# Turned score blocks in layer 2, a last batch with tiles of its own, and dilation counts emitted beside layer 0's end

## The chip, the cores and the metric

One Trainium2 chip, one of its cores. A core has five engines that run side by side, each with a queue that it works off in order: PE (TensorE: matrix products and transposes into PSUM), DVE (VectorE), ACT (ScalarE), POOL (GpSimd) and SP (SyncE, used here to issue loads). Engines wait for each other through semaphores. The metric is the time of one execution on the device, in microseconds, median of several runs.

## The reference

Four layers over a graph with 16 batches of N = 1024 nodes and D = 128 features. Each layer's result is added to its input, and the sum is normalised over the features (mean and variance, epsilon 1e-5).

```python
# layer 0: attention over the symmetrised scores
h = x @ W_w.T + W_b
e = einsum('bjl,bkl->bjk', h @ A, h); e = e + swapaxes(e, 1, 2)
att = softmax(where(adj > 0, e, -9e15), axis=1) * adj
h_prime = relu(att @ h)
coeff = sigmoid(concat([x, h_prime]) @ gate_w.T + gate_b)
return coeff * x + (1 - coeff) * h_prime
# layer 1: dilation (rows one after the other: a row with more than 10 neighbours
# loses those whose rank is a multiple of sf, and the columns likewise), then three
# SAGE convolutions with batch norm on the dilated matrix, and a linear layer on all three
# layer 2: scores as in layer 0 with other weights, but masked with 0:
att = softmax(where(adj > 0, e, 0), axis=1) * adj
h_prime = relu(att @ h)          # three gates i, f, o over concat([x, h_prime])
return o * tanh(sigmoid(i * h_prime + f * x))
# layer 3: two graph convolutions
h = elu(elu(x @ W0 + b0))
norm_A = dinv[:, :, None] * (adj + I) * dinv[:, None, :]   # dinv = (row sum of adj + I) ** -0.5
h = elu(norm_A @ (h @ W1) + b1)
return norm_A @ (h @ W2) + b2
```

As e is symmetric, its block (j, i) is the transpose of block (i, j); the mask is symmetric too.

## The kernel before

P = 128 partitions; a batch's 1024 nodes are NT = 8 row blocks. A [128, 1024] product is made in H2 = 2 halves of 512 columns[...]. The work of one batch is cut into streams, Python generators that emit instructions and pause. `in_rounds` (L816) takes the streams of one round in turns; `yield n` lets a stream pause for n turns. So the order of each engine's queue is mostly written by the pauses, and a scheduler settles the rest and sets the semaphores. A tile's memory is given again to a later tile; the later writer then waits for the last reader.

**Layer 0** (to about 640 us) has three streams in a round: `before(b+1)` loads the adjacency, writes it to fp8 tiles Y (named carry in the trace) that stay on the chip, and sums rows into `deg` (L932); `attention(b)` makes, per row block, a mask (msk, L981), the scores (`wide_matmul`, L724), a reduce that adds the mask and takes the minimum into `mx0` (L984), exp (L986), the scaled rows hs (L990), and, one row block late, the weighted sum acc (L974); `after(b-1)` makes the gates (L1002 to L1011), the mix, the norm (`normed`) and the store to x1_d (L1020, on POOL's queue). After the last round, `after(15)` is emitted alone.

**The dilation** (layer 1's first part) goes through 8 row blocks x 2 groups of 8 batches. `prepare` (L1059) counts neighbours with matmuls (L1078) in two chunks of 4 batches and leaves sk, l1 and past (L1080 to L1084) on DVE; `fixed_point` (L1089) makes 6 evaluations (thr L1101, mid L1106 on DVE, counts pd L1109 on PE, ti L1113), which settle the removed entries of the diagonal block; `removal` (L1142) then works batch by batch on the other columns (first matmul L1153, keep L1157, carry L1166 on ACT). Its pools are opened after layer 0's are closed. Between the first two `prepare` and the loop stand a few operations on layer 0's statistics (L1187 to L1196): mx0 compared and reduced to nomem, deg + 1, its power -1/2 on POOL (dinv is another name for deg), a transpose on PE (L1193), the copy dt and a store. `zeros` is another name for mx0 (L681): layer 2 writes its counts of masked entries there.

**Layer 1's convolutions** follow (to about 1680 us); of their weights, ws (Wr + Wx, in `take_norm`) is touched by the new order.

**Layers 2 and 3** run as one pipeline. In round b: `convolve(b-2)` (layer 3), `mix(b-1)` (layer 2's gates and norm), `attention(b)`, `before(b+1)` (layer 1's linear layer, norm and layer 2's projections). `attention` (L1654), per row block: msk on ACT (L1668), which also sums the mask into zeros, scaled on DVE (L1669); scores on PE (L724); the reduce (add mask, maximum, L1673) from PSUM to em; nmx = -max (L1675); exp in place (L1677); a sum with the masked entries' share (L1680), its reciprocal (L1682), hs (L1684); and, one row block late, acc on PE (L1660). `convolve` (L1726): adjacency copied to fp32r tiles (L1735 ACT, L1745 DVE), transposes of x (x3T, L1739), product with U0 and two elus, then twice: product with U (L1592), split in high and low part (zhi, zlo), product with the adjacency (`propagated`, L1605, DVE L1607). At its end the result is turned back, added (L1771), normalised and stored (L1777, POOL's queue; SP's for the last batch). `before` loads the batch's rows (xn, L1258), makes yT and yn, adds (L1635), normalises, turns (xT, L1640) and multiplies (hT L1644, G L1648, hn L1651). After the rounds `convolve(14)` then `convolve(15)` run as one chain beside `mix(15)`.

A norm is bn_stats (L794) and bn_aggr (L796) on DVE, a power on POOL (L745), one small DVE operation (L799), and ACT's scaling (L801).

Of the kernel before, what the change touches and what calls it, by code (L numbers as in the profile page):

```python
# [9 lines left out]
F32 = mybir.dt.float32  # L10
# [12 lines left out]
P = 128  # L23
# [5 lines left out]
GB = 8  # L29
# [610 lines left out]
def fast_kernel(ctx: ExitStack, tc: tile.TileContext, t: dict, out: bass.AP, flag: bass.AP):  # L640
# [121 lines left out]
    def products(psum, *pairs):  # L762

        for p, c, _ in halves(psum):
            for i, (W, x) in enumerate(pairs):
                nc.tensor.matmul(p, W, x[:, c], start=(i == 0), stop=(i == len(pairs) - 1))  # L766
            yield p, c
# [118 lines left out]
    with ExitStack() as ph:  # L886

        early = ph.enter_context(tc.tile_pool(name="l0_early", bufs=1, reuse_waits="tile"))
        wts = ph.enter_context(tc.tile_pool(name="l0_w", bufs=1, reuse_waits="tile"))
        ps_w = ph.enter_context(tc.tile_pool(name="l0_pw", bufs=2, space=PSUM, reuse_waits="tile"))  # L890
        ps_a = ph.enter_context(tc.tile_pool(name="l0_pa", bufs=1, space=PSUM, reuse_waits="tile"))
        ps_h = ph.enter_context(tc.tile_pool(name="l0_ph", bufs=2, space=PSUM, reuse_waits="tile"))

        with tc.tile_pool(name="l0_raw", bufs=1) as raw:
            W0 = matrix(raw, t["L0_gnn_W_w"], "l0W")
            W0T = transposed(wts, ps_h, W0, "l0WT", "h")
            As0 = symmetric(raw, ps_h, matrix(raw, t["L0_gnn_A"], "l0A"), "l0As", "h")
            AW = raw.tile([P, P], F32, name="l0AW")
            p = ps_h.tile([P, P], F32, name="wtr", tag="h")
            nc.tensor.matmul(p, As0, W0, start=True, stop=True)  # L900
            nc.vector.tensor_copy(AW, p)
            M0 = wts.tile([P, P], F32, name="l0M")
            p = ps_h.tile([P, P], F32, name="wtr", tag="h")
            nc.tensor.matmul(p, W0, AW, start=True, stop=True)
            nc.vector.tensor_copy(M0, p)
            nu = wts.tile([P, 1], F32, name="l0nu")
            p = ps_h.tile([P, 1], F32, name="wtr", tag="h")
            nc.tensor.matmul(p, AW, column(raw, t["L0_gnn_W_b"], "l0b"), start=True, stop=True)
            nc.vector.tensor_scalar(nu, p, -1.0, None, op0=OP.mult)
        work = ph.enter_context(tc.tile_pool(name="l0_work", bufs=1, reuse_waits="tile"))  # L910
        small = ph.enter_context(tc.tile_pool(name="l0_small", bufs=2, reuse_waits="tile"))
        b0 = row_bcast(wts, t["L0_gnn_W_b"], P, "l0brow")
        gw = wts.tile([P, 2, 32], F32, name="l0gw")
        nc.vector.memset(gw, 0.0)
        with nc.allow_non_contiguous_dma(reason="a vector of 256"):
            nc.sync.dma_start(gw[:, :, 0], t["L0_gnn_gate_w"].rearrange("o (h d) -> d (o h)", d=P))
        gb = row_bcast(wts, t["L0_gnn_gate_b"], 1, "l0gb")
        gbh = wts.tile([P, 1], F32, name="l0gbh")
        nc.vector.tensor_scalar(gbh, gb, 0.5, None, op0=OP.mult)
        nbig = wts.tile([P, 1], F32, name="l0nbig")  # L920
        nc.vector.memset(nbig, BIG)

        def before(s, b):

            s.xn = work.tile([P, NT, P], F32, name="xn", bufs=3)
            nc.sync.dma_start(s.xn, nat(t["x"][b]))
            yield 1
            for it in range(NT):
                c = b * NT + it
                an = early.tile([P, N], F32, name="an", bufs=3)  # L930
                nc.sync.dma_start(an, t["adj"][b][it * P:(it + 1) * P, :])
                nc.scalar.activation(Y[b][:, it, :], an, AF.Copy, accum_out=deg[:, c:c + 1], saturate=False)  # L932

                chk = early.tile([P, N], FP8, name="chk")
                done = (it + 1) * P
                if done < N:
                    nc.vector.scalar_tensor_tensor(chk[:, done:], an[:, done:], 0.0, an[:, done:], op0=OP.is_gt,
                                                   op1=OP.not_equal, accum_out=other[:, b, it:it + 1], saturate=False)
                for h in range(it // 4 + 1):
                    js = range(4 * h, min(4 * h + 4, it + 1))  # L940
                    k = slice(js[0] * P, (js[-1] + 1) * P)
                    pt = ps_h.tile([P, 512], F32, name="pt", tag="h")
                    for i, jt in enumerate(js):
                        nc.tensor.matmul(pt[:, i * P:(i + 1) * P], Y[b][:, jt, it * P:done], identb, start=True, stop=True)
                    nc.vector.scalar_tensor_tensor(chk[:, k], pt[:, :k.stop - k.start], 0.0, an[:, k], op0=OP.is_gt,
                                                   op1=OP.not_equal, accum_out=other[:, b, 7 + it + 4 * h:8 + it + 4 * h],
                                                   saturate=False)
                if it == 2:
                    s.xT = work.tile([P, N], F32, name="xT", bufs=2)
                    for p, c, _ in turned(ps_h, s.xn):  # L950
                        nc.scalar.copy(s.xT[:, c], p)
                elif it == 4:
                    s.G = work.tile([P, N], F32, name="G", bufs=2)
                    for p, c in products(ps_h, (M0, s.xT)):
                        nc.scalar.activation(s.G[:, c], p, AF.Identity, scale=-1.0, bias=nu)
                    pz = gates(ps_h, early.tile([P, N], FP8, name="chk").bitcast(F32), (gw[:, 0, :], s.xT))
                    s.gx = small.tile([P, NT], F32, name="gx")
                    nc.vector.tensor_copy(s.gx.rearrange("p (q t) -> p q t", t=2), pz[:, :, :, 0])
                elif it == 5:
                    s.hn = work.tile([P, N], F32, name="hn")  # L960
                    for p, c, blocks in halves(ps_h):
                        for i, k in enumerate(blocks):
                            nc.tensor.matmul(p[:, i * P:(i + 1) * P], s.xT[:, k * P:(k + 1) * P], W0T, start=True, stop=True)
                        nc.vector.tensor_add(tiles3(s.hn[:, c]), tiles3(p), b0[:, None, :].to_broadcast([P, 4, P]))
                yield 2
            nc.gpsimd.dma_start(adj8_d[b], Y[b].bitcast(F32))

        def attention(s, b):
            s.acc = ps_a.tile([P, N], F32, name="acc")

            def weigh(jt, hs, em):
                for h in range(H2):
                    c = slice(h * 512, (h + 1) * 512)
                    nc.tensor.matmul(s.acc[:, c], hs, em[:, c], start=(jt == 0), stop=(jt == NT - 1))  # L974

            for jt in range(NT):
                js = slice(jt * P, (jt + 1) * P)
                c = b * NT + jt
                mn = mx0[:, c:c + 1]
                msk = work.tile([P, N], BF16, name="msk", bufs=2)  # L980
                nc.scalar.activation(msk, Y[b][:, jt, :], AF.Identity, scale=-BIG, bias=nbig)  # L981
                e = wide_matmul(ps_w, s.G[:, js], s.xT)
                em = work.tile([P, N], F32, name="em", bufs=2)
                nc.vector.tensor_tensor_reduce(em, e, msk, 1.0, 3.0e38, op0=OP.add, op1=OP.min, accum_out=mn)  # L984
                sm = small.tile([P, 1], F32, name="sm")
                nc.scalar.activation(em, em, AF.Exp, scale=-1.0, bias=mn, accum_out=sm)  # L986
                rs = small.tile([P, 1], F32, name="rs")
                nc.vector.reciprocal(rs, sm)
                hs = small.tile([P, P], F32, name="hs")
                nc.vector.tensor_scalar(hs, s.hn[:, js], rs, None, op0=OP.mult)  # L990
                yield
                if jt:
                    weigh(*late)
                late = jt, hs, em
                yield
            weigh(*late)
            yield

        def after(s, b):

            hpT = work.tile([P, N], F32, name="hpT")
            nc.scalar.activation(hpT, s.acc, AF.Relu)  # L1002
            yield 3
            pz = gates(ps_h, work.tile([P, NT, P], F32, name="r").rearrange("p t d -> p (t d)")[:, :N // 4], (gw[:, 1, :], hpT))
# [29 lines left out]

# [802 lines left out]
```

## Time and profile before

| what | value |
| --- | --- |
| three runs | 2775.41, 2781.0, 2783.75 us, median 2781.0 |
| the profiled execution | 2779.18 us, its span 2777.5, mean granted TensorE clock 0.978 |
| busy share of the span | PE 93%, DVE 77%, ACT 72%, POOL 12% |
| f32 matmuls of layer 2's scores (L724, G by hT) | 512 records, 593 ns each, 245.0 us |
| reduce of layer 2 (L1673) | 128, 1221 ns each, 156.3 us |
| mask of layer 2 (L1668) | 128, 1150 ns each, and 128 accumulator reads of 192 ns (median) |
| first removal of the dilation | 664.45 us |
| first scores of batch 15 in layer 2 | 2623.35 us |

A line of a timeline or of the page reads: engine, source line, operation, output tile <- input tiles, partitions x elements and type, count; in brackets the time that the engine was idle before it, and what ended that. PE's durations overlap, as matmuls are pipelined: the distance of two starts is what one costs in a full stretch. In the page's section of slices, a digit is the busy share of 1/40 of the span in tenths, and PEclk is the granted clock likewise.

### The profile page before, as it was taken

What the parts mean: (1) busy time and instruction counts of PE and PEld (TensorE: products, weight loads), DVE (VectorE), ACT (ScalarE), POOL (GpSimd) and SP (SyncE); (2) the same over time, 40 slices, a digit from 0 to 9 for tenths busy, and PEclk for the clock granted to TensorE, in tenths of its full rate; (3) what the DMA queues carried; (4) which work ended last, traced back from release to release, by engine and by line L of the source; (5) the groups of instructions that cost most, each with busy time, mean ns of one, the idle gap of its engine ahead of it and who ended that gap; (6) DMA issues with size and microseconds to landing.
All of it is one profiled execution on the core that took longest, in us unless ns stands there. A gap on an engine that the chain in (4) does not pass through costs nothing.

```text
span 2777.5 us, 41717 instructions
## 1 busy us (share of the span) xinstructions
PE 2586.3 (93%) x14808; PEld 1670.4 (60%) x14808; DVE 2131.3 (77%) x5905; ACT 1991.0 (72%) x3316; POOL 334.0 (12%) x287
## 2 busy tenths in 40 slices
PE   7999999995899879998999998999999999999985
PEld 3545444443666658877788894455555555555554
DVE  5888777876999967776788775777778777777865
ACT  6888888974888776666655445877777777777754
POOL 0000000030000002211122141011111111111100
PEclk9999999997999989999999998999999999999998
DMA  5555545520000052233467572111111111121000
GB/s 186 164 162 172 177 161 166 175 89 12 2 2 2 2 219 92 97 117 123 155 235 249 174 267 84 60 62 61 61 61 61 61 61 61 66 68 72 27 20 25
DMA packets 120810, 285.37 MB, mean 103 GB/s; under 512 B 12304, under 2 KB 65424, under 8 KB 113424
## 3 DMA queue, kind: packets, MB, share of 16 engines
q1 hardware_dynamic: 101280, 203.33, 22.3%
q0 software_dynamic: 19312, 79.28, 7.4%
q8 instruction: 119, 1.95, 0.3%
q14 instruction: 99, 0.81, 0.1%
HBM read 202.72 MB, written 79.82 MB: 102 GB/s over the span
## 4 chain that ended last, share of the span: by engine, by line
PE 40%; DVE 19%; ACT 9%; issue 9%; POOL 4%; DMA 3%; POOLq 0%; DVEq 0%; ACTq 0%; SPq 0%
PE pmm L724 6%; PE ph L1605 6%; PE acc L1315 5%; PE acc L1660 5%; PE ph L766 3%; PE ph L759 3%; ACT xn L801 3%; PE acc L974 2%; PE ph L1441 2%; POOL rn L745 2%; DVE em L1673 2%; DVE mid L1106 2%; PE ph L1592 2%; DVE ln_st L794 1%; PE s L1153 1%
## 5 line engine op out<-in xcount | busy, mean ns | idle before, releaser
L745 POOL TENSOR_TENSOR ln_rstd<-ln_rstd,mhalf 128x8 f32<-128x8 f32 (+1 forms) x68 | 121.6, 1788 | 1361.7 <-DVE ln_rstd L742 938.0
L724 PE MATMUL pmm<-xT,G 128*128 128x512 f32 x512 | 261.8, 604 | 0.0
L974 PE MATMUL acc<-em,hs 128*128 128x512 f32 x512 | 260.1, 607 | 1.3 <-DVE hs L990 1.1
L1315 PE MATMUL acc<-a,lo 128*128 128x512 f32 x768 | 240.0, 397 | 17.9 <-DVE lo L1282 17.9
L1660 PE MATMUL acc<-em,hs 128*128 128x512 f32 x512 | 248.6, 601 | 8.1 <-DVE hs L1684 7.8
L724 PE MATMUL pmm<-G,hT 128*128 128x512 f32 x512 | 245.0, 593 | 0.0
L1315 PE MATMUL acc<-a,hi 128*128 128x512 f32 x768 | 240.6, 398 | 3.0 <-ACT hi L1281 2.8
L801 ACT ACTIVATE xn<-xn,ln_nb,ln_rstd 128x128 f32<-128x128 f32 x512 | 205.0, 485 | 48.7 <-DVE ln_nb L799 48.7
L1668 ACT ACTIVATE msk<-A,nbig 128x1024 bf16<-128x1024 fp8e4 x128 | 147.1, 1150 | 73.7 <-DVE mx L1673 48.8
L986 ACT ACTIVATE em<-em,mx 128x1024 f32<-128x1024 f32 x128 | 146.8, 1147 | 59.6 <-DVE mx L984 59.2
L1315 PEld LDWEIGHTS acc<-a,lo 128*128 128x128 f32 x768 | 144.0, 190 | 54.6 <-DVE lo L1282 25.0
L984 DVE CUSTOM_DVE_ANT_0 em<-pmm,msk 128x1024 f32<-128x1024 f32 x128 | 156.3, 1221 | 23.2 <-PE pmm L724 22.4
L1673 DVE CUSTOM_DVE_ANT_0 em<-pmm,msk 128x1024 f32<-128x1024 f32 x128 | 156.3, 1221 | 11.6 <-PE pmm L724 11.3
L1315 PEld LDWEIGHTS acc<-a,hi 128*128 128x128 f32 x768 | 143.4, 190 | 33.1 <-ACT hi L1281 3.7
L1166 ACT ACTIVATE carry<-pc,negone 128x1024 fp8e4<-128x1024 f32 x128 | 141.0, 1115 | 24.4 <-PE pc L1165 19.9
L1605 PE MATMUL ph<-A,zhi 128*128 128x512 f32 x512 | 151.8, 438 | 1.5 <-ACT zhi L1595 1.3
L932 ACT ACTIVATE carry<-an 128x1024 fp8e4<-128x1024 f32 x128 | 134.7, 1052 | 25.9 <-DMA an<-in_adj 25.3
L1677 ACT ACTIVATE em<-em,nmx 128x1024 f32<-128x1024 f32 x128 | 146.2, 1142 | 8.1 <-DVE nmx L1675 7.8
L1660 PEld LDWEIGHTS acc<-em,hs 128*128 128x128 f32 x512 | 90.8, 191 | 92.7 <-issue 69.9
L981 ACT ACTIVATE msk<-carry,l0nbig 128x1024 bf16<-128x1024 fp8e4 x128 | 145.9, 1140 | 0.0
L1304 ACT CAST a<-carry 128x1024 fp32r<-128x1024 fp8e4 x96 | 99.5, 1050 | 50.4 <-PE acc L1315 50.3
L1304 ACT CAST a<-A 128x1024 fp32r<-128x1024 fp8e4 x96 | 99.2, 1050 | 50.3 <-PE acc L1315 50.3
(319 smaller groups left out, 6236.5 us busy)
## 6 DMA issues: line engine op xcount, KB each, us to landing
an<-in_adj SPq DMA_DIRECT2D x128, 512.0 KB, 3.7
adj_d<-carry POOLq DMA_DIRECT2D x16, 1024.0 KB, 4.2
A<-dil_d SPq DMA_DIRECT2D x16, 1024.0 KB, 5.5
rdeg<-rdeg_d SPq DMA_DIRECT2D x32, 512.0 KB, 3.8
A<-adj_d SPq DMA_DIRECT2D x16, 1024.0 KB, 4.8
ag_d<-ag POOLq DMA_DIRECT2D x24, 512.0 KB, 5.2
ag<-ag_d SPq DMA_DIRECT2D x24, 512.0 KB, 5.4
xn<-in_x SPq DMA_DIRECT2D x16, 512.0 KB, 4.3
```

What stands on the lines that cost most here:

```text
L724: nc.tensor.matmul(p[:, h * 512:(h + 1) * 512], lhsT, rhs[:, h * 512:(h + 1) * 512], start=True, stop=True)
L745: nc.gpsimd.tensor_tensor(r, r, mhalf[:, :n], op=OP.pow)
L801: nc.scalar.activation(r[:, k.start + i, :], r[:, k.start + i, :], AF.Identity, scale=rstd[:, i:i + 1], bias=nb[:, i:i + 1])
L974: nc.tensor.matmul(s.acc[:, c], hs, em[:, c], start=(jt == 0), stop=(jt == NT - 1))
L984: nc.vector.tensor_tensor_reduce(em, e, msk, 1.0, 3.0e38, op0=OP.add, op1=OP.min, accum_out=mn)
L986: nc.scalar.activation(em, em, AF.Exp, scale=-1.0, bias=mn, accum_out=sm)
L1304: nc.scalar.copy(a, A[:, 2 * i:2 * i + 2, c])
L1315: nc.tensor.matmul(acc, part[:, jt, :], pieces[h * NT // 2 + i][:, j, :], start=(jt == 0 and p == 0), stop=(jt == NT - 1 and p == 1))
L1605: nc.tensor.matmul(p, part[:, jt, :], A[:, jt, c], start=(jt == 0 and i == 0), stop=(jt == NT - 1 and i == 1))
L1660: nc.tensor.matmul(s.acc[:, c], hs, ex[:, c], start=(jt == 0), stop=(jt == NT - 1))
L1668: nc.scalar.activation(msk, s.A8[:, jt, :], AF.Identity, scale=BIG, bias=nbig, accum_out=zs)
L1673: nc.vector.tensor_tensor_reduce(em, e, msk, 1.0, 0.0, op0=OP.add, op1=OP.max, accum_out=mx)
```

## The change

Three edits.

**Scores.** In layer 2, row block jt multiplies only the columns from (jt - 1) x 128 on. The blocks further left are turned by PE from the masked scores of earlier row blocks, which now stay in two tiles em0 and em1 (even and odd rows, at offsets `starts`). As block and mask are turned together, signs change: G is copied with scale -1, the mask is 0 or +BIG, the reduce takes the minimum, and exp writes to tiles of its own, ex. The mask's sums are gone: zeros is computed once as N - deg, in the dilation's setup. yn has one buffer in place of two; zn, x3T and prop share one tile.

```diff
-                zs = zeros[:, i:i + 1]
-                nc.scalar.activation(msk, s.A8[:, jt, :], AF.Identity, scale=BIG, bias=nbig, accum_out=zs)
-                nc.vector.tensor_scalar(zs, zs, -1.0 / BIG, None, op0=OP.mult)
-                e = wide_matmul(ps_w, s.hT[:, js], s.G)
-                em = wide("em", 3)
-                mx = small.tile([P, 1], F32, name="mx")
-                nc.vector.tensor_tensor_reduce(em, e, msk, 1.0, 0.0, op0=OP.add, op1=OP.max, accum_out=mx)
-                nmx = small.tile([P, 1], F32, name="nmx")
-                nc.vector.tensor_scalar(nmx, mx, -1.0, None, op0=OP.mult)
+                nc.scalar.activation(msk, s.A8[:, jt, :], AF.Identity, scale=-BIG, bias=nbig)
+                e = ps_w.tile([P, N], F32, name="pmm", tag="w")
+                at = max(lo - P, 0)
+                for c in ([slice(at, 512)] if at < 512 else []) + [slice(max(at, 512), N)]:
+                    nc.tensor.matmul(e[:, c], s.hT[:, js], s.G[:, c], start=True, stop=True)
+                for it in range(jt - 1):
+                    nc.tensor.transpose(e[:, it * P:(it + 1) * P], ems[it % 2][:, starts[it] + lo:starts[it] + lo + P], identf)
+                row = ems[jt % 2][:, starts[jt]:starts[jt] + N]
+                mn = small.tile([P, 1], F32, name="mn")
+                nc.vector.tensor_tensor_reduce(row, e, msk, 1.0, 0.0, op0=OP.add, op1=OP.min, accum_out=mn)
                 sm = small.tile([P, 1], F32, name="sm")
-                nc.scalar.activation(em, em, AF.Exp, bias=nmx, accum_out=sm)
+                ex = wide("ex", 2)
+                nc.scalar.activation(ex, row, AF.Exp, scale=-1.0, bias=mn, accum_out=sm)
...
             s.G = wide("G", 2)
             for p, c in products(ps_h, (As2, s.hT)):
-                nc.scalar.copy(s.G[:, c], p)
+                nc.scalar.activation(s.G[:, c], p, AF.Copy, scale=-1.0)
```

**The end of layer 0.** Layer 0's pools are split: `scores` (early and ps_w) closes after the last attention, `ending` after `after(15)`. The dilation's pools open in between, on the right side, and its first two `prepare` and first `fixed_point` are emitted in one round with `after(15)`. The loop starts at 1.

```diff
-        in_rounds([after(state[B - 1], B - 1)])
+    scores.close()
...
-        for s in steps[:G2]:
-            for _ in prepare(*s):
-                pass
+        in_rounds([chain(*(prepare(*s) for s in steps[:G2]), fixed_point(*steps[0])), after(state[B - 1], B - 1)])
+        ending.close()
+        ps_c = ph.enter_context(tc.tile_pool(name="dl_pc", bufs=2, space=PSUM, reuse_waits="tile"))
 
         nc.vector.tensor_scalar(mx0, mx0, 1.0e15, None, op0=OP.is_gt)
         nc.vector.tensor_reduce(nomem, mx0, AX.X, OP.max)
 
+        nc.vector.tensor_scalar(zeros, deg, -1.0, float(N), op0=OP.mult, op1=OP.add)
         nc.vector.tensor_scalar(deg, deg, 1.0, 1.0, op0=OP.add, op1=OP.max)
         nc.gpsimd.tensor_tensor(dinv, deg, mhalf[:, 0:1].to_broadcast([P, BT]), op=OP.pow)
...
-        for i in range(len(steps) + 1):
+        for i in range(1, len(steps) + 1):
```

**The last batch.** A class `Place` names where a batch's layer 3 has its tiles and PSUM: the usual ones, or, for batch 15, those that other streams no longer need, and the PSUM pool of the scores. The rounds run to b = 14, and one last round holds the rest. The pauses are changed: `before` from 1, 3, 7, 1, 4 to 2, 1, 5, 1, 1, `mix`'s last from 5 to 7, and shorter ones for batch 15.

```diff
+        class Place:
+            usual = dict(x="x3T", zhi="zhi", zlo="zlo", dB="dB", e="ehi", eb=2, psum=ps_h, ptag="h")
+            spare = dict(x="yT", zhi="hb2", zlo="yn", dB="em0", e="ex", eb=2, psum=ps_w, ptag="w")
...
+            def adjacency(self):
+                if not self.last:
+                    A = work.tile([P, NT, N], F32R, name="A")
+                    return [A[:, jt, :] for jt in range(NT)]
+                tags = [("hb0", 1), ("hb1", 1), ("hT", 2), ("G", 2), ("hn", 2), ("hT", 2), ("G", 2), ("hn", 2)]
+                return [self.of(f"A{jt}", tag, bufs, F32R) for jt, (tag, bufs) in enumerate(tags)]
...
-        for b in range(B):
+        for b in range(B - 1):
...
-        ends = [chain(convolve(state[B - 2], B - 2), convolve(state[B - 1], B - 1)), mix(state[B - 1], B - 1)]
-        in_rounds(ends)
+        in_rounds([chain(attention(state[B - 1], B - 1), mix(state[B - 1], B - 1), convolve(state[B - 1], B - 1)),
+                   mix(state[B - 2], B - 2),
+                   chain([2], convolve(state[B - 3], B - 3), convolve(state[B - 2], B - 2))])
```

## The prediction

> **What bounds the kernel.** I read the page's 40 slices first, for where an engine is full; then windows of single rounds of layers 2 and 3; then the timeline at the two places where the slices dip.
>
> ```profile
> PE   7999999995899879998999998999999999999985
> ...
> PEclk9999999997999989999999998999999999999998
> ```
>
> One slice is 69.4 us. PE is at 9 nearly everywhere, at full clock; it dips in slice 10 (625 to 694, the seam between layer 0 and the dilation) and in the last two. The change touches just these three regions: the rounds, the seam, the tail. A round of layers 2 and 3, start to start of the same instruction (columns: stretch, length, busy us and count of PE, PEld, DVE, ACT, POOL, then clock, DMA share, GB/s):
>
> ```profile
> 2087.15:2151.20 64.05, 63.57 (x251) 37.16 (x251) 50.17 (x155) 48.48 (x95) 7.06 (x4) 1.00 0.19 66
> 2281.30:2345.40 64.10, 63.63 (x251) 37.22 (x251) 50.23 (x155) 48.55 (x95) 6.75 (x4) 1.00 0.19 66
> ```
>
> PE is busy 63.6 of 64.1 us; DVE 50.2, ACT 48.5. So a round is TensorE time: what PE is spared shortens it, unless a wait appears; what DVE and ACT are spared buys slack only.
>
> **Part 1, scores of layer 2.** In each batch's attention 28 blocks lie under the diagonal. The 7 next to it stay matmuls, the other 21 become transposes of masked blocks kept in em0 and em1. Prices are start-to-start distances in a crowded stretch, since the recorded duration of one matmul overlaps the next:
>
> ```profile
> 2176.43 0.60 PE L759 MATMUL ph<-identf,xn 128*128 128x128 f32 x4
> 2176.87 1.02 PE L724 MATMUL pmm<-G,hT 128*128 128x512 f32 x2
> 2177.73 0.64 PE L759 MATMUL ph<-identf,xn 128*128 128x128 f32 x4
> ```
>
> The x2 of L724 are one 512-column matmul (512 records on the page for 16 batches x 8 row blocks x 2 halves): 0.86 us, 0.215 per 128 columns. Four transposes take 0.44, so 0.109 each. Removed 21 x 0.215 = 4.5 us, added 21 x 0.109 = 2.3: **-2.2 us of PE per batch**.
>
> A rule speaks against this. The Trainium skill, "TensorE: Matmul & The Clock Gate", Part 4 (PE-mode transpose), gives about 275 ns for a 128x128 transpose in a kernel and says that transposes don't by themselves engage the full clock. By it the 21 would cost 5.8 us: +1.3 per batch instead of -2.2. The trace has the same 275 ns as each record's duration (275 mean of L759 over the rounds), but starts 0.109 apart, and the clock of the windows, with 48 transposes in each round, is 1.00. I take 0.109; the new transposes too stand among matmuls, 1 to 6 in a row.
>
> DVE loses 8 x (0.147 for L1669 + 0.148 for L1675) = 2.4 us per round, ACT 8 x 0.193 of accumulator reads = 1.5. Both have over 13 us of slack: nothing, save that the chain from reduce to hs gets 0.15 shorter. Turning signs (min for max, scale -1 on exp and on G's copy) keeps forms and sizes: nothing. The separate ex tiles take exp's output out of em: nothing.
>
> **Stalls in the new round.** The change also moves the streams' pauses, and yn has one buffer for two. In the queue order of the changed kernel, DVE's add onto the next batch's rows (L1635 before) now stands ahead of hs of the third row block; before, three hs were ahead of it. The add waits for a buffer's turn: convolve's result is stored out of it, then the next rows are loaded into it (POOL, SP's queue, DVE):
>
> ```profile
> 2186.09 1.17 POOL L1777 DMA_DIRECT2D out<-xn  x1 [3.73 <-ACT xn L801]
> ...
> 2191.57 0.37 SPq L1258 DMA_DIRECT2D xn<-x_d  x1
> ...
> 2197.80 1.23 DVE L1635 TENSOR_TENSOR xn<-xn,yn 128x1024 f32<-128x1024 f32 x1 [2.59 <-DMA xn<-x_d]
> ```
>
> Store 5.5 us, load 6.2; the add comes 25.2 us after convolve's last product ends (near 2172.6). Add, statistics and aggregation (1.23 + 1.64 + 0.63) and the sums to hs follow: hs of block 2 at 28.7 to 30.5 on that clock, while PE's new queue, added up at the prices above, wants it at 29.0. So 0 to 1.5 us of stall per round, and about 1 at the round's first acc, against some 0.5 that PE idles now (64.05 - 63.57). Ends per round: -2.2 (all covered), 0 (everything eaten). I take -1.5 for each of the 15 rounds, **about -23**; the sixteenth batch's scores are counted in the tail.
>
> **Part 2, the seam.** Before, the dilation's first work waits for after(15)'s store, since its tiles reuse memory:
>
> ```profile
> 648.37 0.16 DVE L1081 SCALAR_TENSOR_TENSOR l<-s,off 128x4 f32<-128x4 f32 x1 [6.47 <-DMA x_d<-xn]
> ...
> 648.85 1.31 PE L1078 MATMUL s<-step,carry 128*128 128x128 bf16 x32 [16.02 <-DVE past L1084]
> ...
> 664.45 1.25 PE L1153 MATMUL s<-step,carry 128*128 128x512 bf16 x4
> ```
>
> PE idles 16 us from 632.8 on, and the first removal starts at 664.45. The change gives the dilation memory of its own on the right side and runs prepare and the six evaluations beside after(15). Taken alone, the evaluations (2.10 us apart: 657.82, 659.92 ...) could end some 15 us earlier. But an operation on POOL, deg to the power of -1/2, is moved with it:
>
> ```profile
> 584.47 20.75 POOL L1191 TENSOR_TENSOR deg<-deg,mhalf 128x128 f32<-128x128 f32 x1
> ```
>
> Before, deg + 1 (L1190) ran early, POOL's 20.75 us were hidden beside attention, and PE turned deg (L1193) at 626.4. Now zeros = N - deg is written over mx0 first, after nomem has read it, which needs the last row block's minimum, and deg + 1 stands behind it on DVE. The last hs is at 626.8; the four small operations (0.2 each) put deg + 1 near 628.5, and the power runs to about 649.5. Three queues stand behind it. PE: the transpose of deg comes right after prepare's second chunk; behind it after(15)'s gates, chunks 3 and 4, all counts. DVE: dt waits for that transpose, behind it all evaluations. POOL: after(15)'s rstd. So work restarts at 649.7, with 6 x 2.10 = 12.6 us of evaluations plus about 9 of after(15) and the last chunks on DVE, of which 2.5 fit in the evaluations' gaps (0.47 each): 19, first removal at 668.8, **+4.5**. One more wait: layer 1's sum of weights is now in DVE's queue within the dilation's first step, and its loads on SP stand behind one that waits for after(15)'s later store (near 680). Between 0 and +3; I take +1.5. Seam: **+6**. If the power were hidden after all, -12; if both waits fall worst, +9. After that step the instructions are in the same order as before.
>
> **Part 3, the tail.** From the first score of batch 15 (2623.35) to the end is 154.2 us. Before, convolve(14), mix(15), convolve(15) share tiles and PSUM (windows as above, then PE's timeline):
>
> ```profile
> 2680.00:2700.00 20.00, 12.30 (x58) 7.83 (x58) 10.14 (x32) 10.97 (x20) 3.07 (x2) 0.73 0.07 26
> ...
> 2720.00:2740.00 20.00, 7.80 (x31) 5.25 (x30) 11.96 (x36) 14.00 (x26) 3.57 (x3) 0.80 0.15 53
> ```
>
> ```profile
> 2738.88 3.55 PE L1592 MATMUL ph<-U,ehi 128*128 128x128 f32 x16 [7.88 <-DVE ehi L1579]
> ...
> 2763.53 0.66 PE L759 MATMUL ph<-identf,prop 128*128 128x128 f32 x4 [1.10 <-ACT prop L1768]
> ```
>
> PE is idle 7.7 and 12.2 us in these windows, some 39 from 2680 on. In the new order batch 15 has tiles and PSUM of its own and runs straight through, with mix(14), convolve(13) and (14) filling in. I add up: first score to last acc 47 us (59 before, because convolve(13)'s last product moves behind it and the scores save 2.2); mix(15) and convolve(15) up to U1, 36 (before 56.7: 2682.2 to 2738.88); then PE is full with both batches' products, 7.35 us each, to +76; and about 20 for the last transposes, norm and store (14.0 before, from 2763.53; batch 14 isn't finely split). 47 + 76 + 20 = 143: **-11**, ends -3 (the chains don't overlap where I assume) and -20 (half the idle time filled).
>
> **Sum.** -23 + 6 - 11 = -28 from the profiled execution's 2779.2 (span 2777.5): 2751. The runs shown have a median of 2781.0, 1.8 above, within their spread.
>
> **Rivals.** Under 0.3% (8.3 us) a measurement of this kernel can't be told from no change.
> A. *As summed*: 2751, own range 2740 to 2766. Chance 0.67.
> B. *The seam isn't blocked*, or the stalls vanish: POOL's power runs early after all, and the seam gains 12 where I count a loss of 6: 2751 - 18 = 2733. For it: the whole gap is one memory wait. Against: the queue order above. 0.20.
> C. *The saved PE time becomes waiting*: the rounds stay at 64 because hs sets the pace: 2779 + 6 - 11 = 2774, no change. For it: the 2.59 us wait at L1635. Against: DVE and ACT have 13 us of slack. 0.08.
> D. *Slower*: those rows arrive later, and PE waits at acc of block 2 in each round. This is a loop: a late round makes the store late again. With 4 us of stall, +1.8 net per round, 15 x 1.8 + 6 - 11 = +22: 2801. It decides from a stall of 2.2 + 5/15 = 2.5 us per round, that is, if the rows land 2.5 us later than I place them. Against: the turn's times are steady (12 rounds within 66.1). 0.05. The skill's transpose price would make it 2779 + 15 x 1.3 + 6 - 7.5 (the tail less its 3.5) = 2797; I count it in here.
>
> Range: 2726 to 2768, from B's far side to half of C. Faster 0.90, same 0.06, slower 0.04.
>
> **What would show it.** Right: rounds of 62.5 to 63 us, PE busy near 61.4; the power on POOL (L1191 before) starting near 628 with PE's transpose of deg after it; first removal at 667 to 672; 140 to 148 us from batch 15's first score to the end. Wrong: DVE idle before the add and PE idle at acc of block 2 by over 1.5 us a round (C, D); four transposes over 0.86 us apart; the first removal before 655 (B).

## The result, and the profile after

The changed kernel takes 2733.9 us (median of 5 runs, 2728.7 to 2735.6) against 2781.0 before: ratio 0.9827, 95% interval 0.9811 to 0.9843, so 47 us less. Forecast were 2751 as the likeliest and 2726 to 2768 as the range. The profiled execution of after has a span of 2732.4 us, 45.1 less than before's 2777.5. Cut at the same instructions of both traces (the first removal of the dilation; the first reduce of batches 0, 3 and 15 in layer 2), the 45.1 are:

| stretch | before | after | difference | forecast |
| --- | --- | --- | --- | --- |
| start to the first reduce of batch 0 (holds the seam) | 1720.8 | 1727.6 | +6.8 | +6 |
| batch 0 to batch 3 | 134.1 | 131.8 | -2.4 | -4.5 |
| batch 3 to batch 15, 12 rounds | 771.3 | 739.1 | -32.2 | -18 |
| first reduce of batch 15 to the end | 151.2 | 133.9 | -17.3 | -11 |

**Rounds.** Windows of two rounds of after (columns as in the prediction), then the whole list of PE's waits in after between 1860 and 2590: total us, times, longest:

```profile
2105.90:2167.50 61.60, 61.28 (x267) 38.31 (x265) 48.89 (x140) 47.83 (x87) 5.86 (x4) 1.00 0.20 69
2290.70:2352.30 61.60, 61.29 (x267) 38.31 (x265) 48.88 (x140) 47.83 (x87) 5.86 (x4) 1.00 0.20 69
```

```profile
PE acc L1678 <- DVE hs L1705: 3.5, 12, 0.3
```

Before, a round took 64.28 us in the mean of 12, between 63.6 and 66.1; now eleven of the twelve take 61.60 to 61.63, and the last 61.46. Over the 12 rounds PE is busy 2.3 us less per round (63.60 to 61.28), about what the turned blocks promised, and its idle time went from 0.7 to 0.3. The one wait left is 0.3 us once per round, at the first acc; the stall at acc of block 2 isn't there. The timeline of POOL, SP's queue and DVE in one round of after shows the add:

```profile
2174.24 0.93 POOL L1799 DMA_DIRECT2D out<-xn  x1 [3.72 <-ACT xn L801]
...
2177.88 0.37 SPq L1249 DMA_DIRECT2D xn<-x_d  x1
...
2184.76 1.22 DVE L1648 TENSOR_TENSOR xn<-xn,yn 128x1024 f32<-128x1024 f32 x1
```

The add has no wait in front of it (no brackets). The rows landed 4.48 us after their issue, at 2182.4, so 2.4 us before it.

**The seam.** The timelines of POOL, then PE, then DVE in after, around 650 us:

```profile
627.96 20.73 POOL L1183 TENSOR_TENSOR deg<-deg,mhalf 128x128 f32<-128x128 f32 x1 [5.87 <-DVE deg L1182]
```

```profile
648.75 0.47 PE L1185 MATMUL pt<-identf,deg 128*128 128x128 f32 x1 [19.12 <-POOL deg L1183]
...
667.54 1.25 PE L1144 MATMUL s<-step,carry 128*128 128x512 bf16 x4
```

```profile
649.26 0.29 DVE L1187 COPY dt<-pt 128x128 f32<-128x128 f32 x1 [18.43 <-PE pt L1185]
```

One operation on POOL holds PE for 19.1 us and DVE for 18.4. The wait for the store of before (6.47 us on DVE, 16.02 on PE) is gone, and this one stands in its place. The first removal comes at 667.54, 3.1 later than before.

**The tail.** Two windows of after, and PE's timeline at the same steps as in the prediction:

```profile
2660.00:2680.00 20.00, 14.12 (x46) 8.73 (x46) 14.93 (x43) 12.98 (x28) 3.85 (x3) 0.82 0.07 27
2680.00:2700.00 20.00, 20.00 (x104) 16.80 (x103) 13.15 (x21) 6.10 (x9) 0.00 (x0) 1.00 0.00 1
```

```profile
2671.05 3.43 PE L1605 MATMUL ph<-U,ehi 128*128 128x128 f32 x16 [3.61 <-DVE ehi L1570]
...
2715.12 1.97 PE L759 MATMUL ph<-identf,prop 128*128 128x128 f32 x8 [3.11 <-ACT prop L1790]
```

From 2680 to 2700 PE is full at full clock: the products of batches 14 and 15 stand side by side. What follows the last transposes at 2715.1 (17.3 us) is batch 14's unsplit end.

### The profile page after: what moved, and what is told of

It reads as the page before. It is cut to its first block, busy times and chain, and to the rows that moved or that the text cites. A ratio compares the mean times of both kernels' runs of the same rounds, so it can differ in the third digit from the quotient of the medians.

```text
span 2732.4 us, 41821 instructions
## 1 busy us (share of the span) xinstructions
PE 2552.2 (93%) x15048; PEld 1688.8 (62%) x15048; DVE 2108.6 (77%) x5650; ACT 1977.0 (72%) x3188; POOL 317.1 (12%) x287
## 4 chain that ended last, share of the span: by engine, by line
PE 62%; DVE 16%; issue 9%; POOL 5%; ACT 4%; DMA 3%; SPq 0%; POOLq 0%; ACTq 0%; DVEq 0%
PE acc L974 8%; PE ph L1618 8%; PE pmm L724 8%; PE acc L1678 7%; PE ph L766 6%; PE acc L1306 5%; PE ph L759 4%; PE pmm L1690 3%; POOL rn L745 2%; PE ph L1605 2%; PE ph L1432 2%; DVE mid L1097 2%; POOL ln_rstd L745 1%; PE s L1144 1%; DVE keep L1148 1%
## 5 line engine op out<-in xcount | busy, mean ns | idle before, releaser
L745 POOL TENSOR_TENSOR ln_rstd<-ln_rstd,mhalf 128x8 f32<-128x8 f32 (+1 forms) x68 | 108.3, 1592 | 1347.6 <-DVE ln_rstd L742 879.7
L974 PE MATMUL acc<-em,hs 128*128 128x512 f32 x512 | 260.1, 607 | 1.9 <-DVE past L1075 1.3
L1678 PE MATMUL acc<-ex,hs 128*128 128x512 f32 x512 | 248.9, 596 | 7.4 <-DVE hs L1705 4.5
L1698 ACT ACTIVATE ex<-em,mn 128x1024 f32<-128x1024 f32 x128 | 146.8, 1147 | 44.6 <-DVE mn L1695 43.9
L1690 PE MATMUL pmm<-G,hT 128*128 128x512 f32 (+3 forms) x416 | 175.3, 523 | 0.1
L1157 ACT ACTIVATE carry<-pc,negone 128x1024 fp8e4<-128x1024 f32 x128 | 140.8, 1114 | 27.0 <-PE pc L1156 21.7
L932 ACT ACTIVATE carry<-an 128x1024 fp8e4<-128x1024 f32 x128 | 134.4, 1050 | 21.7 <-DMA an<-in_adj 20.7
L1618 PE MATMUL ph<-A,hi 128*128 128x512 f32 x512 | 143.1, 420 | 1.2 <-DVE zn L1607 0.7
L1678 PEld LDWEIGHTS acc<-ex,hs 128*128 128x128 f32 x512 | 88.7, 190 | 76.8 <-issue 54.6
```

Of the source, the lines that this page charges most:

```text
L745: nc.gpsimd.tensor_tensor(r, r, mhalf[:, :n], op=OP.pow)
L1618: nc.tensor.matmul(p, part[:, jt, :], A[jt][:, c], start=(jt == 0 and i == 0), stop=(jt == NT - 1 and i == 1))
L1678: nc.tensor.matmul(s.acc[:, c], hs, ex[:, c], start=(jt == 0), stop=(jt == NT - 1))
L1690: nc.tensor.matmul(e[:, c], s.hT[:, js], s.G[:, c], start=True, stop=True)
```

## Experiments

Each was timed against the kernel before in the same series (its median was between 2778.0 and 2781.8). All are edits of the changed kernel. "Round" is the mean of the 12 rounds from batch 3 to batch 15.

| kernel | us | ratio to before, 95% | round | first removal | tail |
| --- | --- | --- | --- | --- | --- |
| changed kernel | 2733.9 | 0.9827 (0.9811 to 0.9843) | 61.59 | 667.5 | 133.9 |
| e1 power early | 2712.2 | 0.9754 (0.9738 to 0.9771) | 61.60 | 647.8 | 134.1 |
| e2 full scores | 2765.0 | 0.9943 (0.9927 to 0.9960) | 63.49 | 668.0 | 136.2 |
| e3 twice turned | 2770.8 | 0.9964 (0.9951 to 0.9976) | 64.00 | 668.8 | 135.6 |
| e4 old pauses | 2743.1 | 0.9868 (0.9851 to 0.9884) | 62.60 | 668.4 | 134.9 |
| e5 mask sums | 2769.2 | 0.9957 (0.9947 to 0.9968) | 64.19 | 668.0 | 141.3 |
| e6 old tail | 2751.6 | 0.9893 (0.9858 to 0.9928) | 61.59 | 668.6 | 151.7 |
| e7 old seam, power early | 2727.0 | 0.9808 (0.9773 to 0.9843) | 61.59 | 665.3 | 134.6 |
| e8 e1 with after(15) first | 2711.0 | 0.9748 (0.9713 to 0.9782) | 61.59 | 653.7 | 134.3 |
| e9 sums alone | 2733.8 | 0.9837 (0.9820 to 0.9854) | 61.60 | 668.6 | 133.4 |
| e10 e8 with a fine end | 2708.4 | 0.9745 (0.9728 to 0.9763) | 61.60 | 653.4 | 130.3 |
| e11 both undone | 2745.7 | 0.9879 (0.9860 to 0.9897) | 62.68 | 669.1 | 137.3 |
| e12 one DVE operation | 2770.1 | 0.9955 (0.9939 to 0.9970) | 64.15 | 668.7 | 141.0 |

### The seam: e1, e7, e8

```diff
+        deg16 = tiny.tile([P, BT], F16, name="deg16", bufs=1)
+        nc.vector.tensor_copy(deg16, deg)
-        nc.vector.tensor_scalar(zeros, deg, -1.0, float(N), op0=OP.mult, op1=OP.add)
+        nc.vector.tensor_scalar(zeros, deg16, -1.0, float(N), op0=OP.mult, op1=OP.add)
```

> The changed kernel, but deg is first copied to a half-precision tile (its counts are whole and at most 1024) and zeros is made from the copy, so that deg + 1 and POOL's power can run early again. If the power was what held the seam: the power starts near 584, the first removal near 650 instead of 667.5 (19 us of DVE work after 631), and the total falls by about 17, to 2717. Rival, after(15)'s own chain through PE, ACT and POOL holds the seam as much: first removal near 660, total 2726 or more.

Measured 2712.2, first removal at 647.8. Timelines of POOL and of PE in e1:

```profile
583.44 20.75 POOL L1185 TENSOR_TENSOR deg<-deg,mhalf 128x128 f32<-128x128 f32 x1
```

```profile
625.41 0.31 PE L1187 MATMUL pt<-identf,deg 128*128 128x128 f32 x1
```

The same 20.75 us are hidden beside attention again, PE's transpose waits for nothing, and 21.7 us come back in the median: more than the 17 expected, and more than the 18 to 19 that PE and DVE stood still. The rival, that after(15)'s own chain would hold the seam, falls.

e7 puts layer 0's end and the dilation's start in the order and memory of before, with the power early through the same copy (its tile in a small pool opened ahead of layer 0):

```diff
-    scores.close()
+    in_rounds([after(state[B - 1], B - 1)])
+    scores.close()
+    ending.close()
...
-        in_rounds([chain(*(prepare(*s) for s in steps[:G2]), fixed_point(*steps[0])), after(state[B - 1], B - 1)])
-        ending.close()
+        for s in steps[:G2]:
+            for _ in prepare(*s):
+                pass
```

> The changed kernel with layer 0's end and the dilation's start as before (after(15) alone, pools opened after it, prepare then the loop from 0), and the power early through a half-precision copy of deg. First removal near 664 as before, no norm scalings ahead of ACT's first q: total 2734 - 7 = 2727. Beside e1 (2712) this gives what running the first counts beside after(15) is worth once the power is out of the way: 15. Rival, it is worth little, and e1's gain is the power alone: total 2715 or less.

Measured 2727.0. So the change's edit at the seam is worth 14.9 us (2727.0 to 2712.2; 13.5 by the traces' stretch to the first reduce of batch 0) once the power is out of its way; the power's new place costs 21.7; the sum, +6.9, is what the changed kernel pays. The old wait is back in e7's DVE timeline:

```profile
648.11 0.49 DVE L1066 TENSOR_TENSOR uY<-carry,upper 128x128 int32<-128x128 int32 x2 [7.46 <-DMA x_d<-xn]
```

e8 is e1 with after(15)'s three pauses at 1, for ACT's eight norm scalings stood ahead of the first q:

```diff
         nc.scalar.activation(hpT, s.acc, AF.Relu)
-        yield 3
+        yield 1 if b == B - 1 else 3
```

> e1 with the pauses of after(15) cut from 3, 3, 4 to 1, 1, 1, so that its norm is through on DVE ahead of most evaluations. If ACT's eight norm scalings (3.2 us) ahead of the first q hold the removals: the first keep comes 4 us after the first removal matmul instead of 7.5, the evaluations lose about 2.4 us of filled gaps, total 2711, 1 less than e1. Rival, the order on DVE alone counts: total 2714 or more.

The first keep came 4.1 us after the first removal matmul instead of 7.5, as expected, but that removal came 5.8 later, and the 17th keep stands at 700.1 against e1's 699.8. The total is 1.1 less, with intervals that overlap: the expected number, but not by the expected way, since the scalings ahead of q did not hold the removals. It looks as if DVE's sum of work sets this stretch whatever its order (from 626.8 to 700 it is busy 62.8 us in e1 and 64.1 in e8), but no run changes that sum alone.

### The rounds: e2, e3, e4

```diff
-                for c in ([slice(at, 512)] if at < 512 else []) + [slice(max(at, 512), N)]:
+                for c in [slice(0, 512), slice(512, N)]:
                     nc.tensor.matmul(e[:, c], s.hT[:, js], s.G[:, c], start=True, stop=True)
-                for it in range(jt - 1):
-                    nc.tensor.transpose(...)
```

> The changed kernel with all 1024 columns of the scores by matmul and no transposes of masked blocks. If a round is PE time and 21 matmul blocks cost 2.2 us more than 21 transposes: rounds of 63.7 to 63.8 instead of 61.60, total up by 16 x 2.2 = 35, to 2769. Rival, the shorter round comes mostly from the moved pauses: rounds under 62.5, total under 2749.

Measured 63.49 and 2765.0. A round of e2, as a window:

```profile
2118.50:2182.00 63.50, 63.43 (x252) 37.38 (x250) 48.90 (x140) 47.74 (x87) 6.70 (x4) 1.00 0.18 66
```

PE is just as full as in after and 2.15 us longer at work. 1.90 us of the round's 2.68 are the turned blocks; the total is 31 higher, of which 2.3 lie in the tail. The rival falls, though 0.8 us per round are left for it.

```diff
-                    nc.tensor.transpose(e[:, it * P:(it + 1) * P], ems[it % 2][:, starts[it] + lo:starts[it] + lo + P], identf)
+                    for _ in range(2):
+                        nc.tensor.transpose(e[:, it * P:(it + 1) * P], ems[it % 2][:, starts[it] + lo:starts[it] + lo + P], identf)
```

> The changed kernel with each transpose of a masked block issued twice, into the same place: 21 more transposes per batch. At the 0.109 us between starts in the trace: rounds 61.6 + 2.3 = 63.9, total up by 37, to 2771. At the 275 ns of the skill's page: rounds 67.4, total up by 92, to 2826.

Measured 64.00 and 2770.8. A stretch as long as one round of e3:

```profile
2100.00:2164.00 64.00, 63.65 (x288) 40.65 (x287) 48.92 (x139) 48.26 (x87) 6.69 (x4) 1.00 0.19 66
```

PE runs 21 instructions more than in after (288 for 267). They cost 2.41 us, 0.115 each. The page's 275 ns (the Trainium skill, "TensorE: Matmul & The Clock Gate", Part 4) is the duration of one record here, not the price of one more among others. Both runs together give the matmul block that was removed: (1.90 + 2.41) / 21 = 0.205 us, against the 0.215 that the prediction took.

```diff
             if b:
                 l2.load(s, b)
-            yield 2
+            yield 1
...
             normed(small, s.xn, b < 2)
-            yield 5
+            yield 7
```

(and the others of `before` and `mix` likewise)

> The changed kernel with the pauses of before in the rounds (before: 1, 3, 7, 1, 4; mix's last 5). If the 0.5 us that PE idled per round before went because of the pauses: idle time returns, rounds of 61.8 to 62.3, total up by 3 to 9. Rival, it went with the shorter PE and DVE work: rounds stay at 61.6 to 61.7.

Measured 62.60 and 2743.1, a little beyond the expected. One round of e4, and the first two lines of PE's waits in it between 1860 and 2590:

```profile
1932.96:1995.40 62.44, 61.78 (x268) 38.28 (x267) 48.38 (x139) 48.17 (x87) 6.94 (x4) 1.00 0.20 68
```

```profile
PE acc L1678 <- DVE hs L1705: 5.3, 12, 0.5
PE ph L759 <- ACT G L1661: 2.0, 11, 0.2
```

So the pauses carry 1.0 us per round. Less than half of it is the idle time that the expectation spoke of: in the mean of 12 rounds PE is idle 0.74 us instead of 0.32, and busy 61.86 instead of 61.28 with the same instructions. Which of the moved pauses does which was not separated.

### What the turned signs took away: e5, e9, e11, e12

The prediction set the removed work of ACT and DVE at nothing. e5 puts it back:

```diff
-                nc.scalar.activation(msk, s.A8[:, jt, :], AF.Identity, scale=-BIG, bias=nbig)
+                zs = zeros[:, i:i + 1]
+                nc.scalar.activation(msk, s.A8[:, jt, :], AF.Identity, scale=-BIG, bias=nbig, accum_out=zs)
+                nc.vector.tensor_scalar(zs, zs, 1.0 / BIG, None, op0=OP.mult)
...
+                nc.vector.tensor_scalar(mn, mn, 1.0, None, op0=OP.mult)
                 sm = small.tile([P, 1], F32, name="sm")
```

> The changed kernel with the mask's sums back on ACT (into zeros, scaled on DVE) and one more small DVE operation between reduce and exp, so with the work of ACT and DVE that the change took away: 1.5 us and 2.4 us per round. If that was slack only: rounds stay at 61.6 and the total within 3 us of 2734. Rival, the chain from reduce to hs was at its edge and this relief is what removed the idle 0.5 us per round: rounds of 62 or more, total up by 6 or more.

Measured 64.19 and 2769.2: 2.60 us per round, more than all the turned blocks (1.90), and against the first of the two expectations. Three runs take it apart.

```diff
-                nc.scalar.activation(msk, s.A8[:, jt, :], AF.Identity, scale=-BIG, bias=nbig)
+                mn = small.tile([P, 1], F32, name="mn")
+                nc.scalar.activation(msk, s.A8[:, jt, :], AF.Identity, scale=-BIG, bias=nbig, accum_out=mn)
```

> The changed kernel with ACT's accumulator reads alone put back (the sum goes to the minimum's column, which the reduce then overwrites): 1.5 us of ACT per round, nothing on DVE. If e5's 2.6 us per round came from the DVE operation between reduce and exp: rounds of 61.6 to 61.7. If they came from ACT's added work: rounds of 63 or more, in pairs of a long and a short one.

Nothing: 61.60 and 2733.8. ACT's eight accumulator reads, 0.19 us each, are slack, as the prediction said. (Their 1.5 us are a sum of records that overlap others: ACT's busy time grew by 0.6 us per round.)

```diff
                 nc.vector.tensor_tensor_reduce(row, e, msk, 1.0, 0.0, op0=OP.add, op1=OP.min, accum_out=mn)
+                nc.vector.tensor_scalar(mn, mn, 1.0, None, op0=OP.mult)
```

> The changed kernel with one small DVE operation (0.15 us) put back between reduce and exp in each row block, and nothing else. If this operation in the chain from reduce to hs is what cost e5 its 2.6 us per round: rounds near 64.2, total near 2769. If it was the other one, the scaling of the mask's sums, which ties DVE to ACT's mask: rounds of 61.6 to 61.8, total within 3 of 2734.

Measured 64.15 and 2770.1, all of e5's loss. Windows of two rounds of e12 that follow each other:

```profile
1985.56:2053.56 68.00, 64.91 (x285) 40.76 (x285) 53.55 (x164) 52.47 (x92) 5.86 (x4) 1.00 0.18 64
2053.56:2113.82 60.26, 58.90 (x247) 35.77 (x245) 45.76 (x130) 43.07 (x82) 5.86 (x4) 1.00 0.20 69
```

Eight operations of 0.15 us on an engine that is idle for 12 us of the round make it 2.55 us longer. The counts tell how: 285 and 247 PE instructions, 164 and 130 on DVE, in turn, where the rounds of after from batch 3 to 13 repeat one sequence on PE, DVE and ACT. With the operation in place, the scheduler's order of the queues settles in a pattern over two rounds. Of the 2.55 us PE is idle 1.9 (2.23 instead of 0.32) and busy 0.6 (61.92 instead of 61.28), and it waits at several places (the first lines of PE's waits in e12, 1860 to 2590):

```profile
PE ph L759 <- ACT prop L1791: 9.8, 11, 1.0
PE acc L1678 <- DVE hs L1706: 6.5, 12, 0.8
PE pmm L1690 <- DVE mn L1695: 2.8, 6, 0.5
```

e11 is e5 with e4's pauses.

> The changed kernel with the mask's sums back as in e5 and with the pauses of before as in e4. If the sums' work is only slack and e5 lost by the order that the new pauses give with it: rounds near e4's 62.6. If the work itself costs PE its feed: rounds of 64 or more as in e5, whatever the pauses.

Measured 62.68 and 2745.7: with the old pauses the same operations cost 0.08 us per round (62.68 against e4's 62.60), and the rounds of e11 repeat one sequence again. So the two edits belong together:

| | old pauses | new pauses |
| --- | --- | --- |
| with the small operations | 62.68 (e11) | 64.19 (e5) |
| without | 62.60 (e4) | 61.59 (after) |

The new pauses alone would lose 1.5 us per round, the missing operations alone gain 0.1, both together gain 1.1. The loss goes with the order that alternates. Whether that order alone does it, or only with the delay of 0.15 us in the chain from reduce to hs, isn't separated: no run had the same order with and without the operation.

### The tail: e6, e10

e6 has before's driver at the end (sixteen rounds, then convolve(14) and convolve(15) in one chain beside mix(15)), its pauses for batch 15, and the usual tiles (`at = Place(False)`).

```diff
-            at = Place(last)
+            at = Place(False)
...
-        for b in range(B - 1):
+        for b in range(B):
...
-        in_rounds([chain(attention(state[B - 1], B - 1), mix(state[B - 1], B - 1), convolve(state[B - 1], B - 1)),
-                   mix(state[B - 2], B - 2),
-                   chain([2], convolve(state[B - 3], B - 3), convolve(state[B - 2], B - 2))])
+        in_rounds([chain(convolve(state[B - 2], B - 2), convolve(state[B - 1], B - 1)), mix(state[B - 1], B - 1)])
```

> The changed kernel with the end of before: sixteen rounds, then convolve(14) and convolve(15) in one chain beside mix(15), with the usual tiles and the pauses of before for batch 15. If the tail's 17 us came from batch 15's own tiles and order: the tail from batch 15's first reduce to the end is 149 (before's 151 less 2.2 of scores) instead of 133.9, total 2749. Rival, the cheaper scores and moved pauses brought most of it: tail under 142, total under 2742.

Measured 2751.6, tail 151.7. That is before's 151.2 again: batch 15's own tiles, order and pauses together are worth 17.7 us, and under the old end the cheaper scores give nothing that shows. In the new order they do: e2's tail is 136.2, 2.3 longer. Which of tiles, order and batch 15's pauses does how much was not separated.

e10 adds to e8 a split end for batch 14:

```diff
+            fine = b >= B - 2
-            for k in spans(last):
+            for k in spans(fine):
...
-                (nc.sync if last else nc.gpsimd).dma_start(nat(out[b])[:, k, :], s.xn[:, k, :])
+                (nc.sync if fine else nc.gpsimd).dma_start(nat(out[b])[:, k, :], s.xn[:, k, :])
```

> e8 with batch 14's end split in two halves like batch 15's (bias, add, norm, and stores on SP's queue), as batch 14 now ends last. If the 20 us behind the last product are one unsplit chain: about 4 to 6 us less, total near 2706. If the store sets the end whatever the split: within 2 of 2711.

Measured 2708.4, tail 130.3 instead of 134.3: 4 us of the tail in the traces, the lower end of the expected. In the total it is not clear of noise: the median is 2.7 less than e8's, but the kernel before was 3.0 less in that series too, and the ratios are 0.9745 (0.9728 to 0.9763) and 0.9748 (0.9713 to 0.9782). Both lie well below the change's 0.9827.

## Why the prediction was right, and where its sizes were off

**The total lies in the range, but not where the sum put it.** 2733.9 is outside the own range of rival A (2740 to 2766) and beside B's 2733. B's first half did not happen: the seam was blocked as summed. Its second, "or the stalls vanish", did, and the tail gave more than summed; that the two together come to what B counted for a free seam is luck. Of the signs named, PE's busy time (61.3), the start of the power (628.0) and the first removal (667.5) came out; the rounds (61.6 for 62.5 to 63) and the tail (138.7 for 140 to 148) went beyond theirs.

**Bound by PE in the rounds: right.** What e2 and e3 added to PE's work moved the round by about as much (2.1 us of busy time for 1.9, 2.4 for 2.4). The forecast of 2.2 us for the turned blocks measured 1.9; the matmul block is 0.205 instead of 0.215, the transpose 0.115 instead of 0.109. The trace's starts, not the page's 275 ns, gave the price.

**The stalls were sized from one round, and it was the worst.** The prediction said "0 to 1.5 us of stall per round, and about 1 at the round's first acc", and took -1.5 where -2.68 came. It placed the add 25.2 us behind convolve's product by the stretch of 2186 to 2198, with a load of 6.1 us and a wait of 2.59. Over before's 12 rounds that load took 3.8 to 6.1, nine of them under 4.4, and the add waited 0.03 to 2.59, in nine of them under 0.8. In after the store took 3.45 to 3.48 us from issue to landing instead of 5.07 to 5.63; the load was no shorter (4.5 to 6.1 in the eleven rounds before the last), but the add waits for it in no round. It stands 23.8 us behind the product, and hs of block 2 ends at 2188.6, before PE wants it at 2189.9. PE's arrival was forecast at 29.0 us on that clock and is 28.9; it is DVE's side that was late in the sum. The stall at the first acc is 0.3 instead of 1.

The rows' arrival is not all that the pauses changed, though: in e4 the add waits under 0.3 us in nine of the twelve rounds, and these too take 62.4 to 62.5 us. Its one wait of 2.08 us stands in a round of 63.9.

**"Nothing" for the turned signs was wrong as a term by itself.** The prediction named the chain's 0.15 us and gave them no price. The reason, slack of 13 us, holds for ACT (e9) and for DVE with the old pauses (e11). With the new pauses the operation between reduce and exp would cost 2.55 us per round (e12). The pauses and this operation together are the -1.1 per round (62.68 to 61.59) that the sum lacked; the scores and buffers with the old pauses, from before's 64.28 to e11's 62.68, give -1.6, close to the -1.5 taken. The sizes of what was taken away were sums of records, too: busy time per round fell by 1.3 us on DVE (50.2 to 48.9) and by 0.7 on ACT (48.5 to 47.8), not by 2.4 and 1.5.

**The seam: right in mechanism, and in size partly by luck.** Power at 628.0 (forecast 628.5) to 648.7 (649.5), first removal 667.5 (668.8), stretch +6.8 (+6). Within it two terms changed places: layer 1's sum of weights ran at 683.4 without holding anything (forecast +1.5), while the dilation fell 6.7 us behind before by its last keep (1021.0 instead of 1014.3), 3.6 more than at the first removal. What remains of after(15) runs in that stretch; that it is the cause was not tested in the changed kernel. The clock isn't it: PE's granted clock is 0.50 behind the first removal in both (664.5 to 672 before, 667.5 to 675 in after). An unblocked seam, as B has it, was priced at -18 against the sum; e1 measured -21.7.

**The tail: right, each step a little too long.** From first score to end 138.7 us instead of 143: last acc after 44.6 (47), U1 of batch 15 after another 32.8 (36), products done at 73.7 (76), the end 20.4 (20). Against 154.2 before this is -15.4 (forecast -11); by the first reduce it is -17.3, as that reduce stands 1.9 us further behind the first score in the new order.

By the cuts of the first table, the total's 17 us beyond the forecast are 12 from the rounds (-34.6 for -22.5) and 6 from the tail, less 1 at the seam.

## What to carry to other kernels

When an edit moves a small computation, follow its longest operation into every queue behind it: a power of 20 us on an idle engine cost 21.7, for want of a buffer of 256 bytes per partition. Size a wait from all rounds of the trace, not from the one that is on the screen. And where a scheduler orders the queues, a small operation in the chain between engines isn't safely priced by its duration (0.15 us cost 2.55 per round, or next to nothing, by the pauses beside it): time it with both sets of pauses, and look at whether each round has the same sequence.

## What the runs showed of the hardware

The time that the 512 KB store at the end of convolve took from issue to landing went with what was issued beside it. In eleven rounds of before, two 512 KB loads of hb followed it by 1.0 and 1.9 us: 5.07 to 5.63 us. In e4 they followed by 1.3 and 2.2 in ten rounds: 4.33 to 4.44; in the eleventh by 1.05 and 1.9: 5.31. In after the first came 3.1 us behind: 3.45 to 3.48. And in the last of the twelve rounds of each, where no hb is left to load: 3.46 or 3.47. So the moved pauses, which issue the loads when the store has nearly landed, took about 1.9 us out of the buffer's turn, which the prediction had carried over from before. The cause is inferred from these times; no run moved the loads alone.

The granted clock was 1.00 in rounds with 71 transposes among the matmuls (after), and with 92 (e3). One more of them cost 0.115 us, where its own record lasts 0.27.
